# Fewer TensorE instructions and 1 MB transfers in the two later passes of a Fourier layer

## The chip, the cores and the metric

The kernel runs on one core of one Trainium2 chip. The core has TensorE for matrix products (its weight loads are listed as PEld beside the matmuls, PE), VectorE (DVE), ScalarE (ACT), GpSimd (POOL) and SyncE (SP), an on-chip memory of 128 partitions, and a smaller one, PSUM, that TensorE writes and VectorE and ScalarE read. Sixteen DMA engines move data between on-chip memory and HBM; instructions on SP, ACT and POOL issue the transfers. The metric is the device time of one execution in microseconds, smaller is better.

## The reference

Images of 256 x 256 points (64 of them) go through a Fourier neural operator with 32 channels and four layers; its output, joined with 77 text rows, goes through attention and a feed-forward layer. The change lies in the four layers:

```python
v = jnp.transpose(h @ p_w + p_b, (0, 3, 1, 2))            # 64 x 32 x 256 x 256
for i in range(4):
    x_ft = jnp.fft.rfft2(v)                               # 12 x 24 modes are kept
    x1 = irfft2(modes of x_ft, mixed over channels by fw1[i], fw2[i])
    x2 = jnp.einsum('bcxy,cd->bdxy', v, w_w[i]) + w_b[i]
    v = x1 + x2
    v = (v - mean) * rsqrt(var + eps) * bn_g[i] + bn_b[i] # mean, var over images and points
    if i < 3: v = relu(v)
out = einsum('bcxy,cu->bxyu', v, q_w) + q_b
```

Everything is fp32. The mean and variance are taken over all images, so that each layer needs a pass over all data before the next can normalise.

## The kernel before

An image's activation v is 32 channels x 65,536 points, 8 MB, and lives in HBM in two sets of buffers (`vd`), as eight chunks of 1 MB: 128 partitions x 8 rows x 256 values. `layer` (line 546) is one pass over the 64 images. It is called three times, with i = 0, 1, 2; between passes `mix` (line 428) multiplies the kept modes by the weights. In pass 0 nothing is loaded but the small input image; in passes 1 and 2, "the later passes", every chunk is loaded from one set of buffers and stored to the other.

For image b and chunk t a pass has these steps, each a small function of `layer`:

- `am` (643): SP loads the mixed modes of image b (`ams`), and POOL scales them in place (`scale_am`, 631).
- `sp`, `spT` (658, 667): inverse transform along x on PE, then a transpose on DVE into `y`.
- `ld` (652): load of the chunk into `vin`, four buffers.
- `pre` (676): on PE, the inverse transform along y (line 682, 8 products of 256 columns) plus the channel product of the loaded chunk (line 693, 16 products on 32 x 32 tiles of the array, 512 columns each), into two PSUM tiles.
- `evA`, `evB` (700): each evicts one of the two PSUM tiles with relu into `vo`, four buffers; the letter `a` or `d` behind the point picks ACT (705) or DVE (707).
- `st` (711): store of the chunk `vo`.
- `turn` (716): DVE transposes the chunk for the forward transform.
- `prod` (724): PE multiplies the chunk by the next layer's channel weights (line 730, 16 products on 32 x 32 tiles), and `sqA`, `sqB` (736) let ACT square and sum the result, for the variance.
- `y0` to `y7` (745): forward transform along y on PE (752), one eighth of it each; `half`, `zt0`, `zt1` (759, 765) move and transpose the result.
- `x` (778): forward transform along x on PE: 12 products with full 128 x 128 weights taken from `zt` and 96 columns of the table FX (line 786). `xo` (795) copies the result, `xs` (802) has SP store it.

An fp32 product is two pairs of weight load and matmul in the profile.

The order of all steps is written out by hand in two strings, `ORDER[0]` for pass 0 and `ORDER[1]` for the later passes (line 128). A word such as `evA2.a@1` is step evA for chunk 2 of image b+1, on ACT; the loop at line 824 walks the string once for each b. Each engine executes its instructions in this order. PSUM is four tiles called `ring`: `pre`, `prod` and `y` take two each, `sp` and `x` one, and `close` frees them in order. Both `ld` and `st` split a chunk in two halves of 512 KB, and both are issued on SP, hence into one queue. Waits are put in by the framework: a load waits for the product that read its buffer's former content, an eviction for the store of its buffer's former content.

The lines of the steps above that matter most in what follows:

```python
nc.sync.dma_start(vin[b, t][:, rows], src[b][:, t, rows])       # 656, twice per chunk
nc.sync.dma_start(dst[b][:, t, rows], vo[b, t][:, rows])        # 714, twice per chunk
for k in range(4):                                              # 727, prod
    for n in range(4):
        j = (n + k) % 4
        nc.tensor.matmul(ps[n][32 * j:32 * j + 32], lhsT=w4[i + 1][32 * n:32 * n + 32], ...)
```

Of the kernel before, what the change touches and what calls it, by code (L numbers as in the profile page):

```python
# [9 lines left out]
F32 = mybir.dt.float32  # L10
# [7 lines left out]
C = 32  # L18
M = 12
KX = 2 * M  # L20
# [14 lines left out]
def _tables():  # L35
# [92 lines left out]
ORDER = [(  # L128
# [7 lines left out]
), (  # L136
# [7 lines left out]
)]  # L144

_TABLES, _GRIDS = _tables()
# [7 lines left out]
def tile_fno_fusion_transformer(ctx: ExitStack, tc: tile.TileContext, a, cst_d, grid_d, out):  # L154
    nc = tc.nc
    x = a["x"].rearrange("b x y o -> b x (y o)")
# [3 lines left out]
    const = ctx.enter_context(tc.tile_pool(name="const", bufs=1))  # L160
# [15 lines left out]
    T4, ID, ONES, CHAN = tab("t4"), tab("ident"), tab("ones"), tab("chan")  # L176

    CROW = tab("crow").rearrange("p (n k) -> p n k", n=4)

    epsc = const.tile([128, 1], F32, name="epsc")  # L180
    nc.vector.memset(epsc, EPS)

# [29 lines left out]
    w4 = [w4all[:, i, :] for i in range(L)]  # L212
# [333 lines left out]
    def layer(i, st, src, dst, acc):  # L546
# [3 lines left out]
        EX, FX = EXL[lay], FXL[lay]  # L550
# [3 lines left out]
        with ExitStack() as cx:  # L554
            def pool(name, bufs, **kw):
                return cx.enter_context(tc.tile_pool(name=name, bufs=bufs, **kw))

            ip = pool("li", 2 if i == 0 else 4, reuse_waits="tile")
            op, yp, cp, xp, zp, tp = (
                pool(n, k, reuse_waits="tile")  # L560
                for n, k in (("lo", 4), ("ly", 1), ("lc", 1), ("lx", 2), ("lz", 1), ("lt", 6))
            )
# [20 lines left out]
            for n in range(nr):  # L583
# [4 lines left out]
                if n:  # L588
                    nc.vector.tensor_add(a0, a0, a1)
            nc.vector.tensor_copy(ams[1], ams[0])  # L590
            ws = cp.tile([128, C], F32, name="ws")
            if i:
                nc.vector.tensor_mul(ws, w4[i], s_)
            if i == 0:
                mv = [ip.tile([128, 4, 4 * S + 8], F32, name="mv") for n in range(2)]
                mv = [t[:, :, 0:4 * S].rearrange("p q (s y) -> p q s y", s=4) for t in mv]
                for t in mv:
                    nc.sync.dma_start(t, grid_d.rearrange("p (q s y) -> p q s y", q=4, s=4))

            ring, free, clock = {}, [0] * 4, [0]  # L600

            def take(key, n):

                clock[0] += 1
                mine = sorted((k for k in range(4) if free[k] >= 0), key=lambda k: free[k])[:n]
                for k in mine:
                    free[k] = -1
                ring[key] = [(k, pp.tile([128, 2, 512], F32, name=f"ring{k}")) for k in mine]
                return [t for _, t in ring[key]]

            def banks(key):
                return [t[:, n] for _, t in ring[key] for n in range(2)]

            def close(key, n):

                clock[0] += 1
                free[ring[key][n][0]] = clock[0]

            y_, t32, vin, vo, half_, zts = {}, {}, {}, {}, {}, {}
# [31 lines left out]

            def ld(b, t, e):
                vin[b, t] = ip.tile([128, 8, S], F32, name="vin")
                for n in range(2):
                    rows = slice(4 * n, 4 * n + 4)
                    nc.sync.dma_start(vin[b, t][:, rows], src[b][:, t, rows])

            def sp(b, h, e):
                ps = take(("sp", b, h), 1)[0]
# [49 lines left out]
                return run  # L709

            def st_(b, t, e):
                for n in range(2):
                    rows = slice(4 * n, 4 * n + 4)
                    nc.sync.dma_start(dst[b][:, t, rows], vo[b, t][:, rows])
# [9 lines left out]
            def prod(b, t, e):  # L724
                take(("prod", b, t), 2)
                ps = banks(("prod", b, t))
                for k in range(4):
                    for n in range(4):
                        j = (n + k) % 4
                        nc.tensor.matmul(  # L730
                            ps[n][32 * j:32 * j + 32], lhsT=w4[i + 1][32 * n:32 * n + 32],
                            rhs=vo[b, t][32 * n:32 * n + 32, 2 * j:2 * j + 2, :], start=True, stop=True,
                            skip_group_check=True, tile_position=(32 * n, 32 * j),
                        )

            def sq(n):
                def run(b, t, e):
                    key = "prod", b, t
                    at = 2 * (8 * b + t) + n
                    ps = ring[key][n][1]  # L740
                    nc.scalar.activation(ps, ps, AF.Square, accum_out=acc[:, at:at + 1])  # L741
                    close(key, n)
                return run
# [21 lines left out]
            def zt(h):  # L765
                def run(b, n, e):
                    if b not in zts:
                        zts[b] = zp.tile([128, 2, 32, C], F32, name="zt")
                    whole = h == 0 or b not in half_
                    nc.vector.transpose(  # L770
                        zts[b][:, h].rearrange("p k c -> p c k"),
                        (ring["y", b][h][1] if whole else half_[b]).rearrange("p n (s c) -> p c (n s)", c=C),
                    )
                    if whole:
                        close(("y", b), h)
                return run

            def x_(b, n, e):
                zt_ = zts.pop(b)
                ps = take(("x", b), 1)[0]  # L780
                for g in range(3):
                    n = 0
                    for h in range(2):
                        for r in range(2):
                            k0 = M * r + 4 * g
                            nc.tensor.matmul(  # L786
                                ps[:, 0, 96 * g:96 * g + 96],
                                lhsT=zt_[:, h, k0:k0 + 4, :].rearrange("p k c -> p (k c)"),
                                rhs=FX[:, h, 48 * r:48 * r + 96], start=n == 0, stop=n == 3,
                            )  # L790
                            n += 1

            xos = {}

            def xo(b, n, e):
                xos[b] = xp.tile([128, 3, 2 * KX], F32, name="xo")
                nc.scalar.copy(
                    xos[b], ring["x", b][0][1][:, 0, 0:288].rearrange("p (g k) -> p g k", g=3)[:, :, 0:2 * KX]
                )
                close(("x", b), 0)  # L800

            def xs(b, n, e):
                nc.sync.dma_start(xh_d[i][:, b, :], xos.pop(b).rearrange("p g k -> p (g k)"))

            run = dict(
                am=am, lx=lx, ld=ld, sp=sp, spT=spT, pre=pre, evA=ev(0), evB=ev(1), st=st_, turn=turn,
                prod=prod, sqA=sq(0), sqB=sq(1), y=y, half=half, zt0=zt(0), zt1=zt(1), x=x_, xo=xo, xs=xs,
            )
            steps = []
            for word in ORDER[min(i, 1)].split():  # L810
                word, _, late = word.partition("@")
                word, _, e = word.partition(".")
                name = word if word in run else word.rstrip("0123456789")
# [48 lines left out]
    src = vd[L % 2]  # L862
# [50 lines left out]
    with tc.tile_pool(name="tw", bufs=1) as tp, tc.tile_pool(name="tq", bufs=2, space=PSUM) as tq:  # L913
# [5 lines left out]
        for dh in range(2):  # L919
            ps = tq.tile([128, D], F32, name="wtp")  # L920
# [5 lines left out]
        for l, r, d_ in ((wn["q"], wn["k"], wqk), (wn["v"], woT, wvE[:, :, 0:D])):  # L926
            for dh in range(2):
                ps = tq.tile([128, D], F32, name="wtp")
                for eh in range(2):
                    nc.tensor.matmul(  # L930
                        ps, lhsT=l[:, eh, 128 * dh:128 * dh + 128], rhs=r[:, eh, :],
                        start=eh == 0, stop=eh == 1,
                    )
                evict(d_[:, dh, :], ps)
        for dh in range(2):
            ps = tq.tile([128, D], F32, name="wtp")
            for eh in range(2):
                nc.tensor.matmul(
                    ps[:, 0:1], lhsT=wn["k"][:, eh, 128 * dh:128 * dh + 128], rhs=bcol["q"][:, eh, :],
                    start=eh == 0, stop=eh == 1,  # L940
# [4 lines left out]
        ps = tq.tile([128, D], F32, name="wtp")  # L945
# [4 lines left out]
    rows = [128, 128, TXT]  # L950
# [283 lines left out]
```

## Time and profile before

| | us |
|---|---|
| median of 3 runs | 11281.18 (11275.21 to 11285.59) |
| the profiled execution | 11293.58 |
| its span | 11291.7 |
| PE busy | 10625.0 (94%) |
| DVE busy | 8446.5 (75%) |
| ACT busy | 6473.1 (57%) |
| POOL busy | 1442.4 (13%) |

The page cuts the span into 40 equal slices; each digit is the busy share of a slice in tenths, and the last row gives what the DMA engines moved:

```profile
PE   6999999998999999999799999999996999999999
DVE  6888888887777777777677777777775666666665
DMA  6776676678999999999899999999998555555553
GB/s 213 247 250 244 249 247 248 246 253 320 383 376 382 380 377 372 374 379 379 305 375 380 380 376 378 381 380 376 372 379 291 226 227 228 227 227 228 226 227 140
```

Pass 0 fills slices 1 to 8, the two later passes slices 9 to 29 (the dips at 19 and 30 are the mixing between them), and the transformer with its own loads of v the rest. DMA engines read and write at about 380 GB/s in the later passes. Matmuls are pipelined and their ends are modelled in the trace, so PE's share says less than the other rows.

### The profile page before, as it was taken

How to read it: one execution, taken by the hardware profiler on the slowest of the kernel's cores; microseconds unless marked ns; L12 is line 12 of the kernel's file. 1: busy time of each engine (PE TensorE's matmuls, PEld its weight loads, DVE VectorE, ACT ScalarE, POOL GpSimd, SP SyncE). 2: the span in 40 equal slices, each digit the busy share in tenths (PEclk: the TensorE clock that was granted, in tenths of full speed). 3: DMA queues.
4: the chain of work that ended last, by engine and by line, in shares of the span. 5: the costliest groups of instructions: out<-in, count | busy, mean ns of one | idle time of the engine just before them, and what ended most of it. 6: DMA issues, size and time to landing. Idle time of an engine off the chain costs nothing.

```text
span 11291.7 us, 409300 instructions
## 1 busy us (share of the span) xinstructions
PE 10625.0 (94%) x182550; PEld 5738.0 (51%) x182550; DVE 8446.5 (75%) x10381; ACT 6473.1 (57%) x10673; POOL 1442.4 (13%) x2179
## 2 busy tenths in 40 slices
PE   6999999998999999999799999999996999999999
PEld 3555555554444444444444444444443666666666
DVE  6888888887777777777677777777775666666665
ACT  5777777775566655566555566655563333333333
POOL 1111111110000000000000000000000333333333
PEclk8999999998999999999899999999998999999999
DMA  6776676678999999999899999999998555555553
GB/s 213 247 250 244 249 247 248 246 253 320 383 376 382 380 377 372 374 379 379 305 375 380 380 376 378 381 380 376 372 379 291 226 227 228 227 227 228 226 227 140
DMA packets 972544, 3457.29 MB, mean 306 GB/s; under 512 B 149784, under 2 KB 199320, under 8 KB 903832
## 3 DMA queue, kind: packets, MB, share of 16 engines
q1 hardware_dynamic: 905344, 3366.80, 77.8%
q0 software_dynamic: 58288, 60.60, 2.3%
q8 instruction: 1428, 23.40, 0.8%
q10 hardware_dynamic: 7144, 3.72, 0.1%
q14 instruction: 340, 2.79, 0.1%
HBM read 1733.60 MB, written 1696.92 MB: 304 GB/s over the span
## 4 chain that ended last, share of the span: by engine, by line
PE 62%; DMA 20%; DVE 9%; ACT 3%; issue 3%; SPq 2%; POOL 0%; ACTq 0%; DVEq 0%; POOLq 0%
PE ring L752 15%; DMA v<-vo 11%; PE ring L682 9%; PE ring L730 8%; DMA vin<-v 6%; PE ring L693 5%; PE hp L982 4%; PE ring L662 3%; PE pp L1145 3%; PE pp L1156 3%; PE ring L786 2%; DVE vo L707 2%; PE pp L1110 2%; PE pp L1175 2%; PE pp L1072 1%
## 5 line engine op out<-in xcount | busy, mean ns | idle before, releaser
L741 ACT ACTIVATE ring<-ring 128x1024 f32<-128x1024 f32 x3072 | 3115.8, 1014 | 1188.4 <-PE ring L730 1119.5
L719 DVE STREAM_TRANSPOSE t<-vo 128x2048 f32<-128x2048 f32 x1536 | 3465.7, 2286 | 20.9 <-DVE vo L707 0.9
L730 PE MATMUL ring<-vo,w 32*32 32x512 f32 x49152 | 2413.1, 600 | 85.0 <-ACT vo L705 68.3
L707 DVE TENSOR_SCALAR vo<-ring 128x1024 f32<-128x1024 f32 x1280 | 1544.5, 1221 | 1199.7 <-PE ring L693 806.6
L705 ACT ACTIVATE vo<-ring 128x1024 f32<-128x1024 f32 x1792 | 1791.7, 1023 | 1044.1 <-PE ring L693 500.9
L752 PE MATMUL ring<-t,cst 32*32 32x512 f32 x49152 | 2072.0, 599 | 51.0 <-issue 44.9
L752 PEld LDWEIGHTS ring<-t,cst 32*32 32x32 f32 x49152 | 913.4, 103 | 925.6 <-issue 622.6
L730 PEld LDWEIGHTS ring<-vo,w 32*32 32x32 f32 x49152 | 803.2, 103 | 1070.2 <-issue 407.1
L693 PE MATMUL ring<-vin,ws 32*32 32x512 f32 x32768 | 1287.8, 603 | 22.9 <-issue 16.2
L682 PE MATMUL ring<-cst,y 24*128 24x256 f32 x16384 | 1230.3, 402 | 77.0 <-DVE vo L707 61.7
L682 PEld LDWEIGHTS ring<-cst,y 24*128 24x128 f32 x16384 | 789.5, 185 | 993.2 <-DVE vo L707 392.4
L631 POOL TENSOR_TENSOR ams<-ams,bns 48x512 f32<-48x512 f32 x384 | 400.5, 1043 | 6989.4 <-DMA ams<-mix 6510.1
L670 DVE STREAM_TRANSPOSE y<-ring 128x1024 f32<-128x1024 f32 x384 | 763.1, 1987 | 329.5 <-PE ring L662 328.5
L682 PE MATMUL ring<-mv,y 29*128 29x256 f32 x8192 | 705.3, 403 | 36.3 <-ACT ring L741 19.6
L682 PEld LDWEIGHTS ring<-mv,y 29*128 29x128 f32 x8192 | 456.9, 185 | 369.0 <-ACT ring L741 209.3
L786 PEld LDWEIGHTS ring<-cst,zt 128*128 128x128 f32 x4608 | 533.6, 193 | 177.1 <-ACT vo L705 114.2
L762 ACT COPY half<-ring 128x1024 f32<-128x1024 f32 x192 | 194.4, 1013 | 731.4 <-PE ring L752 731.4
L1183 POOL DMA_DIRECT2D out_dram<-o x1024 | 508.2, 505 | 659.0 <-DVE o L1178 616.9
L741 ACT ACTIVATION_READ_ACCUMULATOR ring<-ring 128x1 f32 x3072 | 585.6, 191 | 0.0
L786 PE MATMUL ring<-cst,zt 128*128 128x96 f32 x4608 | 565.6, 280 | 6.1 <-DVE zt L770 5.7
L770 DVE STREAM_TRANSPOSE zt<-ring 128x1024 f32<-128x1024 f32 x192 | 377.4, 1965 | 248.1 <-PE ring L752 248.1
L662 PE MATMUL ring<-ams,cst 49*128 49x512 f32 (+1 forms) x1536 | 450.6, 642 | 99.1 <-POOL ams L631 37.2
(374 smaller groups left out, 9762.6 us busy)
## 6 DMA issues: line engine op xcount, KB each, us to landing
v<-vo SPq DMA_DIRECT2D x3072, 512.0 KB, 7.8
vin<-v SPq DMA_DIRECT2D x2048, 512.0 KB, 9.1
ch<-v SPq DMA_DIRECT2D x512, 1024.0 KB, 12.5
mix<-ob SPq DMA_DIRECT2D x96, 512.0 KB, 5.6
ams<-mix SPq DMA_DIRECT2D x384, 96.0 KB, 8.0
xin<-in_x_dram SPq DMA_DIRECT2D x16, 1024.0 KB, 6.5
mv<-in_x_dram POOLq DMA_DIRECT2D x256, 64.0 KB, 7.4
out_dram<-o POOLq DMA_DIRECT2D x1024, 16.0 KB, 3.0
```

The source lines that it names most:

```text
L662: nc.tensor.matmul(ps[:, n, :], lhsT=EX[hv, 128 * h:128 * h + 128], rhs=ams[b % 2][hv], start=True, stop=True, skip_group_check=True,)
L670: nc.vector.transpose(y_[b, h].rearrange("p q c -> p c q"), ring[key][0][1].rearrange("p n (c k) -> p (n c) k", k=32),)
L682: nc.tensor.matmul(ps[n][:, 256 * r:256 * r + 256], lhsT=y_[b, t // 4][32 * n:32 * n + K, q:q + 4, :].rearrange("p q c -> p (q c)"), rhs=m ...
L693: nc.tensor.matmul(ps[n][32 * j:32 * j + 32], lhsT=ws[32 * n:32 * n + 32], rhs=v[32 * n:32 * n + 32, 2 * j:2 * j + 2, :], start=False, sto ...
L705: nc.scalar.activation(to, ring[key][h][1], AF.Relu)
L707: nc.vector.tensor_scalar(to, ring[key][h][1], 0.0, None, ALU.max)
L719: nc.vector.transpose(t32[b, t // 2][:, :, 8 * (t % 2):8 * (t % 2) + 8, :].rearrange("p y s c -> p s y c"), vo[b, t].rearrange("p s (y l) ...
L730: nc.tensor.matmul(ps[n][32 * j:32 * j + 32], lhsT=w4[i + 1][32 * n:32 * n + 32], rhs=vo[b, t][32 * n:32 * n + 32, 2 * j:2 * j + 2, :], st ...
L741: nc.scalar.activation(ps, ps, AF.Square, accum_out=acc[:, at:at + 1])
L752: nc.tensor.matmul(ps[n][32 * j:32 * j + 32], lhsT=FYT[32 * n:32 * n + 32, k, :], rhs=t32[b, j][32 * n:32 * n + 32, k].rearrange("p s c -> ...
L786: nc.tensor.matmul(ps[:, 0, 96 * g:96 * g + 96], lhsT=zt_[:, h, k0:k0 + 4, :].rearrange("p k c -> p (k c)"), rhs=FX[:, h, 48 * r:48 * r + ...
L1183: nc.gpsimd.dma_start(out[b, 64 * n + 16 * g:64 * n + 16 * g + 16].rearrange("(p t) d -> p t d", t=2), o[32 * g + 8 * n:32 * g + 8 * n + 8 ...
```

## The change

Only passes 1 and 2 are touched, apart from two small tables.

- A chunk is loaded by one 1 MB transfer on SP instead of two of 512 KB.
- A chunk is stored by one 1 MB transfer, issued on GpSimd instead of SP.
- The x transform takes its weights from the table FX and streams `zt` through the array: 4 products of 384 columns, each into 64 PSUM partitions. The result then lies the other way round; `xe` copies it to on-chip memory and `xt` turns it with 3 products against `ID2`, two stacked unit matrices that also add the two halves.
- Two of an image's eight `prod` steps (chunks 1 and 7, marked `.w`) use 8 products on 64 x 64 tiles with the block-diagonal weights `w64`, instead of 16 on 32 x 32 tiles.
- `ORDER[1]` is written anew.

```diff
-    "pre5 sqB7@-1 zt1@-1 sqA7@-1 pre6 evA5.a ld2@1 st4 evB5.d st5 turn4 evA6.a prod5 x@-1 "
-    "evB6.a sqB5 prod6 sqA5 xo@-1 turn5 pre2@1 sqA6 turn6 sqB6 prod4 evA2.a@1 evB2.d@1 "
-    "sqB4 ld0@1 ld7 sqA4 pre0@1 evB0.d@1 ld3@1 prod2@1 st6 evA0.a@1 turn2@1 sqB2@1 sqA2@1 "
-    "pre3@1 ld1@1 evA3.a@1 st2@1 evB3.d@1 pre7 evB7.d prod3@1 ld5@1 evA7.a sqA3@1 turn7 "
-    "pre1@1 st0@1 am@2 sqB3@1 prod0@1 evA1.a@1 evB1.d@1 sqA0@1 st7 sp1@1 st1@1 ld4@1 y0 "
-    "spT1@1 y1 ld6@1 turn0@1 turn3@1 xs@-2 y2 sqB0@1 prod1@1 y3 sqB1@1 sp0@2 y4 sqA1@1 "
-    "spT0@2 y5 y6 st3@1 turn1@1 y7 half.a pre4@1 zt0 prod7 evB4.d@1 evA4.a@1 "
+    "evB2.a@1 ld5 ld7 pre4 ld0@1 turn6 evA2.a@1 prod6 evA4.a x@-1 evB4.d xe.d@-1 turn4 "
+    "sqB6 prod4 xt@-1 st2@1 sqA6 turn2@1 sqA4 pre5 xo@-1 sqB4 am@2 evA5.d evB5.a pre3@1 "
+    "prod2@1 evA3.d@1 turn5 evB3.a@1 st4 xs@-1 sqA2@1 pre7 sqB2@1 evA7.a prod5 evB7.d "
+    "sqB5 pre0@1 st5 ld1@1 sqA5 prod3@1 turn7 evB0.a@1 sp1@1 sqA3@1 evA0.d@1 pre1@1 "
+    "sqB3@1 spT1@1 evA1.a@1 prod0@1 sqA0@1 ld6@1 evB1.d@1 ld2@2 st3@1 sp0@2 spT0@2 y0 "
+    "ld4@1 y1 st1@1 sqB0@1 turn3@1 turn0@1 pre6@1 y2 y3 evA6.a@1 y4 evB6.a@1 prod1.w@1 "
+    "sqB1@1 st7 sqA1@1 y5 st0@1 y6 st6@1 turn1@1 y7 prod7.w half.a zt0 sqA7 sqB7 ld3@2 "
+    "zt1 pre2@2 "
...
+    ID2 = const.tile([128, 2 * KX], F32, name="id2")
+    nc.vector.tensor_add(ID2, ID[:, 0:2 * KX], ID[:, 64:64 + 2 * KX])
...
+            w64 = cp.tile([128, 2, C], F32, name="w64")
+            nc.vector.memset(w64, 0.0)
+            for n in range(4):
+                nc.vector.tensor_copy(w64[32 * n:32 * n + 32, n % 2, :], w4[i + 1][32 * n:32 * n + 32])
+            w64 = w64.rearrange("p n o -> p (n o)")
...
             def ld(b, t, e):
-                for n in range(2):
-                    rows = slice(4 * n, 4 * n + 4)
-                    nc.sync.dma_start(vin[b, t][:, rows], src[b][:, t, rows])
+                nc.sync.dma_start(vin[b, t], src[b][:, t])
...
             def st_(b, t, e):
+                if i:
+                    nc.gpsimd.dma_start(dst[b][:, t], vo[b, t])
+                    return
...
             def prod(b, t, e):
+                if e == "w":
+                    for j in range(4):
+                        for n in range(2):
+                            m = (n + j) % 2
+                            nc.tensor.matmul(
+                                ps[j][64 * m:64 * m + 64], lhsT=w64[64 * n:64 * n + 64],
+                                rhs=vo[b, t][64 * n:64 * n + 64, 2 * j:2 * j + 2, :], start=True, stop=True,
+                                skip_group_check=True,
+                            )
+                    return
...
             def x_(b, n, e):
+                if turned:
+                    for r in range(2):
+                        for h in range(2):
+                            nc.tensor.matmul(
+                                ps[64 * h:64 * h + 64, 0, 0:384], lhsT=FX[:, h, 48 * r:48 * r + 64],
+                                rhs=zt_[:, h, M * r:M * r + M, :].rearrange("p k c -> p (k c)"),
+                                start=r == 0, stop=r == 1, skip_group_check=True,
+                            )
+                    return
...
+            def xe(b, n, e):
+                xes[b] = xp.tile([128, 384], F32, name="xe")
...
+                    nc.vector.tensor_copy(xes[b], ring["x", b][0][1][:, 0, 0:384])
+
+            def xt(b, n, e):
+                xe_ = xes.pop(b)
+                for g in range(3):
+                    nc.tensor.matmul(
+                        ring["x", b][0][1][:, 1, 96 * g:96 * g + 2 * KX],
+                        lhsT=xe_[:, 128 * g:128 * g + 128], rhs=ID2, start=True, stop=True,
+                    )
```

`xo` copies its 288 columns from the PSUM tile's other bank when the transform is turned. In pass 0 all steps stay as they were.

More of the change, by code (lines that the diff above doesn't have):

```diff
@@ L598, in layer @@
                     nc.sync.dma_start(t, grid_d.rearrange("p (q s y) -> p q s y", q=4, s=4))
+            turned = "xt" in ORDER[min(i, 1)]
             ring, free, clock = {}, [0] * 4, [0]
@@ L791, in x_ @@
                             n += 1
-            xos = {}
+            xos, xes = {}, {}
+            def xe(b, n, e):
+                xes[b] = xp.tile([128, 384], F32, name="xe")
+                if e == "a":
+                    nc.scalar.copy(xes[b], ring["x", b][0][1][:, 0, 0:384])
+                else:
+                    nc.vector.tensor_copy(xes[b], ring["x", b][0][1][:, 0, 0:384])
[6 more added lines that the diff above has]
+                    )
             def xo(b, n, e):
@@ L797, in xo @@
                 nc.scalar.copy(
-                    xos[b], ring["x", b][0][1][:, 0, 0:288].rearrange("p (g k) -> p g k", g=3)[:, :, 0:2 * KX]
+                    xos[b], ring["x", b][0][1][:, int(turned), 0:288].rearrange("p (g k) -> p g k", g=3)[:, :, 0:2 * KX]
                 )
@@ L806, in layer @@
                 am=am, lx=lx, ld=ld, sp=sp, spT=spT, pre=pre, evA=ev(0), evB=ev(1), st=st_, turn=turn,
-                prod=prod, sqA=sq(0), sqB=sq(1), y=y, half=half, zt0=zt(0), zt1=zt(1), x=x_, xo=xo, xs=xs,
+                prod=prod, sqA=sq(0), sqB=sq(1), y=y, half=half, zt0=zt(0), zt1=zt(1), x=x_, xe=xe,
+                xt=xt, xo=xo, xs=xs,
             )
```

## The prediction

> **What bounds the kernel now.** I began with the forty slices on the page: one stage, slices 9 to 29, runs with the DMA share at nine tenths. These are the two later passes (lines 546 to 827 with i = 1 and 2), the only ones the change alters. Next I asked for busy time by window, for one steady window of each stage. Columns: window, length, busy us and instruction count of TensorE (PE), its weight loads (PEld), VectorE (DVE), ScalarE (ACT), GpSimd (POOL), then clock, DMA share, GB/s.
>
> ```profile
> core 0: us, PE busy (x) PEld busy (x) DVE busy (x) ACT busy (x) POOL busy (x), PEclk, DMA share, GB/s
> 3000.00:5000.00 2000.00, 1915.77 (x40768) 902.98 (x40766) 1496.18 (x835) 1199.22 (x1888) 91.91 (x88) 1.00 0.98 377
> 300.00:2400.00 2100.00, 2042.04 (x38758) 1073.14 (x38758) 1867.73 (x1039) 1600.59 (x2536) 248.25 (x346) 1.00 0.70 247
> ```
>
> First row, a later pass: DMA 0.98 and PE 96% at once. Second row, the first pass: PE is 97% "busy" with a third less DMA, so a busy PE here proves little (matmul ends are modelled), while 16 engines at 98% cannot be pressed further. Of x transforms 44 fall into the 2000 us, so one image takes 45.45 us; 2 passes x 64 images make 128 images, and **1 us per image is 128 us**.
>
> The DMA view and the waits of the same window:
>
> ```profile
> q1 hardware_dynamic: 214437, 749.15, 96.9%
> vin<-v SPq DMA_DIRECT2D x704, 512.0 KB, 9.0
> v<-vo SPq DMA_DIRECT2D x702, 512.0 KB, 8.9
> ams<-mix SPq DMA_DIRECT2D x88, 96.0 KB, 8.6
> ```
> ```profile
> ACT vo L705 <- DMA v<-vo: 95.7, 71, 3.0
> DVE vo L707 <- DMA v<-vo: 94.3, 72, 3.0
> PEld ring L693 <- DMA vin<-v: 9.0, 18, 1.0
> POOL ams L631 <- DMA ams<-mix: 1861.2, 43, 46.1
> ```
>
> One queue carries everything, and a half-chunk takes 9 us to land though its bytes alone need 1.3 us: a deep queue. Evictions wait for a vo buffer whose store is still under way, (95.7 + 94.3) / 44 = 4.3 us per image; both halves of a chunk wait together, so about 2.2 us of path. Loads are almost never waited for. The chain of waits over one image, however, stays on PE:
>
> ```profile
> by line: PE ring L682 22.9%; PE ring L693 21.7%; PE ring L752 21.2%; PE ring L730 17.1%; PE ring L786 6.5%; DVE vo L707 5.5%; PE ring L662 5.2%; issue 1.1%
> ```
>
> So two limits lie close together. From the matmul records, time from the start of a group to the next one's, at its tenth percentile: L682 1.08 us, L693 0.88, L730 1.07, four y groups 4.44, x 2.85, sp 1.06. Per image 8 x (1.08 + 0.88 + 1.07) + 2 x 4.44 + 2.85 + 2 x 1.06 = 38.1 us of PE, 7.3 under the period. DMA: the window's packets sum to 44.5 us per image, 0.9 under it. DMA is the tighter.
>
> **1 MB transfers.** A chunk row of 4 KB is now 8 KB. Packet records of the window: 4096 B take 159 ns at the median, 168.1 in the mean. Per image 4096 of them: 4096 x 168.1 / 16 engines = 43.0 us. No 8192 B packet flows in this stage. Nearest row for the loads: ch in the last stage, SyncE, 1 MB, same rows: 313 ns median, 320.4 mean. For the stores: xh, loaded through GpSimd in 32,256 B packets of 1194 ns; with 159 for 4096 that is 27.2 B/ns plus 8.5 ns a packet, so 309.6 ns for 8192. Under load either the excess of 9 ns stays per packet (318.6) or it grows in proportion (327). Savings per image, 2048 x (336.2 - t) / 16: 2.25 us at 318.6, 1.18 at 327; 0.6 if only the loads get long packets. I take 1.18, since the ch row was measured in an unsaturated stage, and add the 16 dropped DMAs, a 9 ns completion packet on each engine: 0.14. Together **1.3 us**.
>
> The Trainium skill ("DMA: Bandwidth & Descriptors", Measured) says to batch to 1 MiB for 75% of peak, with about 2.0 us fixed plus bytes / 436 GB/s per DMA. By that, 32 half-MB DMAs would take 32 x 3.2 = 102 us per image and 16 whole ones 71; the trace has 45.45 and 377 GB/s already. The fixed part is covered by the queue here; only the packet's 8.5 ns counts.
>
> **Stores on GpSimd.** The same page ("Issuing engines are not separate DMA queues") speaks against a gain: all issuers share 16 engines and only sequencer time is saved. I agree: SP is freed of 16 issues and of its waits for evictions (368.4 us, 8.4 per image), but loads were waited for only 9 us in all, so that is worth nothing. The cost on POOL is this row:
>
> ```profile
> L845 POOL DMA_DIRECT2D xh<-xh x3: 552/552/557, 2532.8 to 8569.7; - x3
> ```
>
> 0.55 us each, 8 per image = 4.4 us, beside 2.1 us of scaling in 45: idle time. But POOL runs in order, and `am` makes it wait for the ams loads before it scales; `st4` and `st5` now queue behind. That is new:
>
> ```profile
> 5042.03 1.56 SPq L623 DMA_DIRECT2D ams<-mix  x2
> ```
> ```profile
> 5051.63 2.17 POOL L631 TENSOR_TENSOR ams<-ams,bns 48x512 f32<-48x512 f32 x2 [42.67 <-DMA ams<-mix]
> ```
>
> Issue to end of scaling is 11.8 us. In the new order SP issues `am` right after `ld0`, which waits for `pre4`; so `st4` leaves at about pre4 + 12.4. Its vo buffer is wanted by the fourth next chunk, `pre0`: between lie prod6, x, prod4, xt, pre5, pre3, prod2, pre7, prod5, pre0, about 14.6 us at the floors, 17.4 at the stage's ratio 45.45 / 38.1. If the store lands within 5 us nothing is lost; in 6.4 us (1 MB at half the rate, 5.1, plus the 1.3 by which the fastest half-chunk, 2.6, exceeds its bytes) 1.4 are exposed; with today's 8.9, 3.9. Bounds 0 to 3.9. I take 0: freed of stores, the queue ahead of ams is shorter, and work-conserving engines load meanwhile.
>
> **x transform.** 24 matmul instructions (12 fp32 products of two passes each) in 2.85 us go. Added: 4 products of 384 columns on half the array's columns, two side by side, and 3 turns of 48 columns against ID2. The 512-column passes step by 0.43 us, so 384 take 0.32; two pairs x two passes = 1.28, plus a 0.2 us switch. The turns are 6 instructions at 2.85 / 24 = 0.12: 0.7, plus 0.2. Together 2.4: **0.45 saved**. `xe.d` is a 384-column PSUM read on DVE, by L707 (1.22 us for 1024) 0.5 us; DVE gives one eviction to ACT (7 to 6 on DVE), so is less loaded; prod4 stands between xe and xt and hides it; without that cover PE would lose the 0.5.
>
> **Two wide products.** 16 instead of 32 matmuls each, but only four 64x64 tiles work at once instead of sixteen: 4 rounds x 0.43 = 1.71 us against 1.07. The tiling page ("TensorEngine Tiling (Array Packing)", Key Properties) adds that changing the mode drains the array; the rows price that: sp needs 2 rounds x 0.43 = 0.85 and takes 1.06, so 0.2 each way. By rounds alone +0.64, with drains +1.04 each. Against it: narrow groups run at 1.07 where their stream needs 0.85, that is 64 instructions at 16.7 ns, so PE is bound by issue there; 32 fewer give back 0.53 if they queue up behind the wide one. Between +0.1 and +1.04; I take 0.5 each, +1.0 per image. PE in sum: +0.55 on 38.1. It lies in PE's 7.3 us of slack except where a ring waits behind it: 0.2 counted.
>
> **Order, tables.** The order is written anew; both sides keep four buffers. SP now issues only loads, ams and xs: each `ld` still waits for the chunk four places earlier (ld0 for pre4, ld1 for pre3, ld6 for pre5), and no longer behind an eviction. Before, a load took 9.0 us to land from a queue that it shared; after, ld5 leaves before pre4 and pre5 starts some 6 us later (prod6, x, prod4, xt: 4.9 at the floors), with one load ahead instead of a mixed queue. Bounds: the 9 us that loads cost in 44 images, 0.2 each, could go (gain 0.2), or pre5 could wait 9.0 - 6 = 3 us; nearest is the L693 row, so 0. The earlier `pre2@2` adds one chunk of run-in: under 3 us per pass. ID2 and w64 are a handful of VectorE instructions per pass: under 2 us in all.
>
> **Sum.** 1.3 - 0.2 = 1.1 us per image x 128 = **141 us**. The profiled execution took 11293.6 (span 11291.7 and 1.9 around it): 11153. It lies 12.4 above the median 11281.2, so against that: **11140**.
>
> **Rivals.**
> A, the forecast: DMA paces the stage. For it: 0.98 and the waits for stores. Against: the chain never leaves PE and VectorE. 11140; own range 0.4 to 2.2 us per image: 11000 to 11230. Chance 0.47.
> B, PE's order binds: the relief is unused, wide products cost up to their drains, 2.1 - 0.45 = 1.6 us, about half hidden, 0.8: 11281 + 102 = 11383; with all hidden, no change. For it: the chain. Against: 7.3 us of slack, and PE stops on evictions that wait for stores. Chance 0.15.
> C, slower: `st4` and `st5` stuck behind the scaling, vo comes free late, pre0 and pre1 wait. Exposed 1.4 to 3.9, middle 2.6, less 1.1 gained = +1.5 us: 11281 + 192 = 11473. It decides the sign from 1.1 us exposed. For it: the 11.8 us, and stores are already what is waited for. Against: while stores are held, the engines serve loads, and a backlog is made up at full rate. Chance 0.38.
>
> Only 0.2% can be told from no change, 23 us. Faster takes A (0.47); the same gets 0.08 from B and C's edge; slower 0.45. The range reaches from A's stronger half to most of C: 11010 to 11440.
>
> **What would show it.** Packets of 8192 B in both queues near 320 ns and a DMA share under 0.98 with a shorter period show the first step. "vo <- DMA v<-vo" per image under 4.3 us favours A, over it C, with POOL's stores starting right after the scaling. Groups of wide products: 1.7 to 2.1 us; x and turns 2.4. Period near 44.3 us. I am wrong if packets stay 4 KB, or if the period rises with POOL's stores bunched.

## The result and the profile after

The changed kernel takes 12466.97 us in the median of 4 runs (12459.09 to 12470.66), the kernel before 11279.12 beside it: ratio 1.1051, 95% interval 1.1038 to 1.1065. It is **10.5% slower**; 141 us less had been forecast, 1188 more came. Over 128 images of the later passes that is 9.3 us each.

The page after, in the forty slices (counted from 0):

```profile
PE   6999999978888888888788888888888799999999
DMA  6767676778888888888788888888887755555553
```

The later passes now fill slices 9 to 31 of a longer span. PE and DMA both fell from 9 to 8 there: neither of the two is what sets the time now. The same steady window as before, with the same columns:

```profile
3000.00:5000.00 2000.00, 1682.91 (x32040) 715.40 (x32027) 1200.87 (x689) 1023.06 (x1594) 228.76 (x363) 0.91 0.82 312
```

POOL executes ten instructions per image (eight stores, two scalings), so 363 of them are 36.3 images: 55.1 us per image, where it was 45.45. The clock is down to 0.91. Then the DMA view of the window (packets, MB and share; issues with the median from issue to landing) and its waits (us in total, times, longest):

```profile
q1 hardware_dynamic: 51579, 314.06, 43.7%
q0 software_dynamic: 41904, 305.15, 37.8%
...
v<-vo POOLq DMA_DIRECT2D x291, 1024.0 KB, 10.4
vin<-v SPq DMA_DIRECT2D x290, 1024.0 KB, 6.2
ams<-mix SPq DMA_DIRECT2D x72, 96.0 KB, 9.5
```
```profile
ACT vo L712 <- DMA v<-vo: 288.4, 37, 10.4
DVE vo L714 <- DMA v<-vo: 282.8, 37, 10.2
PE ring L689 <- ACT vo L712: 274.2, 37, 9.9
POOL ams L640 <- DMA ams<-mix: 272.2, 33, 10.7
```

The transfers did what they say: 8192 B packets in both queues, 309 ns at the median. But evictions wait for a store once per image, 288.4 / 36.3 = 7.9 us of it; both halves of the chunk wait at the same time, and PE (L689) waits behind them. One image in the timeline (start, length, engine and line; in brackets the idle time before and what ended it):

```profile
5026.22 0.53 POOL L720 DMA_DIRECT2D v<-vo  x1 [14.83 <-ACT vo L712]
5026.54 0.89 SPq L632 DMA_DIRECT2D ams<-mix  x2
...
5036.20 2.16 POOL L640 TENSOR_TENSOR ams<-ams,bns 48x512 f32<-48x512 f32 x2 [9.45 <-DMA ams<-mix]
...
5037.99 1.16 PE L700 MATMUL ring<-vin,ws 32*32 32x512 f32 x32
...
5038.32 1.64 POOL L720 DMA_DIRECT2D v<-vo  x3
...
5045.89 1.02 ACT L712 ACTIVATE vo<-ring 128x1024 f32<-128x1024 f32 x1 [6.66 <-DMA v<-vo]
5045.90 1.22 DVE L714 TENSOR_SCALAR vo<-ring 128x1024 f32<-128x1024 f32 x1 [6.85 <-DMA v<-vo]
...
5046.97 2.29 PE L689 MATMUL ring<-cst,y 24*128 24x256 f32 x16 [6.54 <-ACT vo L712]
...
5049.19 2.01 PE L700 MATMUL ring<-vin,ws 32*32 32x512 f32 x32
```

`st2` leaves, SP issues the load of `ams`, and GpSimd stands still for 9.45 us until it lands. Chunk 4 has been in `vo` since 5027.4, but `st4`, `st5` and `st3` leave only behind the scaling, in one bunch at 5038.32: a ready store was held 10.9 us. Chunk 7's products (5037.99) are done at 5039.15, and its evictions wait until 5045.9, when the first store of the bunch has landed. Then two PE groups take 2.29 and 2.01 us instead of the 1.15 and 1.16 that the same lines take elsewhere in this image. The windows around the wait give the reason (the last three numbers are clock, DMA share, GB/s):

```profile
5036.00:5040.00 4.00, 4.00 (x111) 1.62 (x93) 3.06 (x2) 2.84 (x5) 3.68 (x5) 1.00 1.02 420
5040.00:5044.00 4.00, 0.42 (x15) 0.00 (x0) 0.00 (x0) 0.00 (x0) 0.00 (x0) 1.00 1.00 369
5044.00:5047.00 3.00, 0.03 (x2) 0.04 (x2) 1.10 (x1) 1.11 (x2) 0.00 (x0) 0.57 1.00 401
5047.00:5049.00 2.00, 2.00 (x16) 1.54 (x16) 1.90 (x2) 1.97 (x4) 0.00 (x0) 0.50 1.02 430
5049.00:5050.00 1.00, 1.00 (x20) 0.28 (x32) 0.54 (x1) 0.00 (x0) 0.00 (x0) 0.50 1.01 426
5050.00:5051.00 1.00, 1.00 (x33) 0.27 (x2) 0.00 (x0) 0.00 (x0) 0.00 (x0) 0.50 0.61 246
5051.00:5052.00 1.00, 1.00 (x48) 0.46 (x31) 0.65 (x1) 0.59 (x1) 0.00 (x0) 0.88 0.10 41
```

All engines are still while the DMA engines work at full rate; the clock drops to 0.50 and stays there until about 5051; and when the bunch and the queued loads are through, the DMA engines in turn have nothing to do (0.10): loads wait for buffers that only a running PE frees (in the window SP's load instructions wait 1698.4 us in all for PE's channel products, line 700).

### The profile page after: what moved, and what is told of

It reads as the page before. It is cut to its first block, busy times and chain, and to the rows that moved or that the text cites. A ratio compares the mean times of both kernels' runs of the same rounds, so it can differ in the third digit from the quotient of the medians.

```text
span 12463.5 us, 394621 instructions
## 1 busy us (share of the span) xinstructions
PE 10980.0 (88%) x177174; PEld 5617.4 (45%) x177174; DVE 8338.7 (67%) x10397; ACT 6593.1 (53%) x10801; POOL 1989.6 (16%) x3203
## 5 line engine op out<-in xcount | busy, mean ns | idle before, releaser
L712 ACT ACTIVATE vo<-ring 128x1024 f32<-128x1024 f32 x1920 | 1917.6, 1023 | 2642.7 <-PE ring L700 1472.3
L714 DVE TENSOR_SCALAR vo<-ring 128x1024 f32<-128x1024 f32 x1152 | 1391.8, 1217 | 1529.3 <-DMA v<-vo 920.0
L689 PE MATMUL ring<-cst,y 24*128 24x256 f32 x16384 | 1420.1, 436 | 933.2 <-ACT vo L712 877.9
L750 PE MATMUL ring<-vo,w 32*32 32x512 f32 x40960 | 1931.4, 623 | 29.6 <-ACT vo L712 28.1
L689 PEld LDWEIGHTS ring<-cst,y 24*128 24x128 f32 x16384 | 911.4, 201 | 1769.5 <-ACT vo L712 993.9
L720 POOL DMA_DIRECT2D v<-vo x1024 | 549.5, 541 | 5009.6 <-ACT vo L712 4892.9
L772 PEld LDWEIGHTS ring<-t,cst 32*32 32x32 f32 x49152 | 849.8, 103 | 1103.9 <-issue 746.4
L750 PEld LDWEIGHTS ring<-vo,w 32*32 32x32 f32 x40960 | 663.4, 105 | 922.1 <-issue 495.9
L689 PE MATMUL ring<-mv,y 29*128 29x256 f32 x8192 | 702.5, 402 | 36.9 <-ACT ring L761 19.8
L689 PEld LDWEIGHTS ring<-mv,y 29*128 29x128 f32 x8192 | 454.2, 184 | 370.2 <-ACT ring L761 212.8
L741 PE MATMUL ring<-vo,w 64*64 64x512 f32 x4096 | 521.8, 610 | 8.0 <-issue 6.7
L1027 PE MATMUL hp<-ch,win 128*32 128x512 f32 x4096 | 471.8, 601 | 7.4 <-DMA ch<-v 7.2
## 6 DMA issues: line engine op xcount, KB each, us to landing
ch<-v SPq DMA_DIRECT2D x512, 1024.0 KB, 12.4
```

The source lines that it names most:

```text
L689: nc.tensor.matmul(ps[n][:, 256 * r:256 * r + 256], lhsT=y_[b, t // 4][32 * n:32 * n + K, q:q + 4, :].rearrange("p q c -> p (q c)"), rhs=m ...
L712: nc.scalar.activation(to, ring[key][h][1], AF.Relu)
L714: nc.vector.tensor_scalar(to, ring[key][h][1], 0.0, None, ALU.max)
L720: nc.gpsimd.dma_start(dst[b][:, t], vo[b, t])
L741: nc.tensor.matmul(ps[j][64 * m:64 * m + 64], lhsT=w64[64 * n:64 * n + 64], rhs=vo[b, t][64 * n:64 * n + 64, 2 * j:2 * j + 2, :], start=Tr ...
L772: nc.tensor.matmul(ps[n][32 * j:32 * j + 32], lhsT=FYT[32 * n:32 * n + 32, k, :], rhs=t32[b, j][32 * n:32 * n + 32, k].rearrange("p s c -> ...
```

## The experiments

The ratio is always to the kernel before, run beside each experiment (its medians lie between 11279 and 11284 us); differences between two medians are divided by 128 images.

**e1: the scaling behind the stores.** `am` in the later passes only loads; a new word `sm` scales behind `st3`, three stores further on in GpSimd's queue.

```diff
-    "... evB1.d@1 ld2@2 st3@1 sp0@2 ..."
+    "... evB1.d@1 ld2@2 st3@1 sm@2 sp0@2 ..."
             def am(b, n, e):
                 if b > 1:
                     load_am(b)
-                    scale_am(b)
+                    if not i:
+                        scale_am(b)
+            def sm(b, n, e):
+                if b > 1:
+                    scale_am(b)
```

> The changed kernel with the scaling of ams moved, in the later passes, from its place at am@2 (ahead of st4 and st5 on GpSimd) to a place behind st3@1; the load stays where it is. Held stores (GpSimd waits 7.5 us per image for the ams load, three stores behind it leave together and evictions wait for them): the stall of 7.8 us per image goes, period about 46 us, time 11,250 to 11,500. Slow stores (a 1 MB store from GpSimd takes 10.4 us to land wherever it stands): no more than 2 us per image gained, time above 12,200. Slow order or wide products: the same, above 12,200.

11236.75 us, ratio 0.9961 (0.9946 to 0.9976). The whole loss is gone, 9.6 us per image, and a small gain stands. Window and waits as above:

```profile
3000.00:5000.00 2000.00, 1967.88 (x39571) 844.28 (x39570) 1481.97 (x847) 1262.00 (x1961) 283.20 (x444) 1.00 0.96 383
```
```profile
POOL v L725 <- DMA ams<-mix: 19.3, 13, 1.6
ACT vo L717 <- DMA v<-vo: 14.8, 17, 2.2
```

GpSimd's timeline over one image:

```profile
5000.44 0.53 POOL L725 DMA_DIRECT2D v<-vo  x1 [13.29 <-ACT vo L717]
5002.15 0.53 POOL L725 DMA_DIRECT2D v<-vo  x1 [1.18 <-DVE vo L719]
5009.57 0.53 POOL L725 DMA_DIRECT2D v<-vo  x1 [6.89 <-DVE vo L719]
5011.59 0.53 POOL L725 DMA_DIRECT2D v<-vo  x1 [1.48 <-PE ring L755]
5012.19 2.16 POOL L640 TENSOR_TENSOR ams<-ams,bns 48x512 f32<-48x512 f32 x2
```

`st2`, `st4`, `st5` and `st3` leave one by one as their chunks come. The scaling comes 11.75 us behind `st2`, where it came 9.98 behind it before: hardly later in time, but with nothing held and hardly a wait of its own (19.3 us in the whole window). 44.4 images, 45.05 us each; the clock is 1.00 and evictions wait 0.3 us per image.

The balance of the loss, 55.1 - 45.05 = 10.05 us per image, has two parts. PE stands still longer: from its busy time in the two windows, (2000 - 1682.91) / 36.3 = 8.7 us per image against (2000 - 1967.88) / 44.4 = 0.7, so 8.0 more. And PE works at half clock for a while: the clock records of the trace show 9.5 us per image at 0.50, in 5.6 of which PE is busy, and half of that is lost, an estimate of 2.8 (e1 has none). In the image shown the second part is smaller, 1.14 + 0.85 = 2.0. Together 10.8, slightly more than the whole.

**e5: a dose.** The scaling between `st4` and `st5`, so that `st4` is free and `st5` and `st3` are held.

```diff
-    "... evB3.a@1 st4 xs@-1 ..."
+    "... evB3.a@1 st4 sm@2 xs@-1 ..."
```

> Dose: the changed kernel with the scaling between st4 and st5, so that st4 leaves freely and st5 and st3 are held. Held stores: pre0 no longer waits, but pre1 wants the buffer of st5, which leaves about 4 us late, so a part of the stall comes back, some 1 to 4 us per image over the 44.8 of the first experiment: 11,350 to 11,750. If any place of the scaling but the original one were harmless (a peculiarity of that one place): 11,230 to 11,250.

11499.01, ratio 1.0193 (1.0177 to 1.0208): 2.0 us per image over e1, with 142.2 us of waits in 42.4 images, 3.4 each. Holding the later stores costs a fifth of holding the first.

**e9: the other end of the wait.** Scaling stays ahead of `st4`, but SP issues the load one round of the order earlier (`al@3` behind `st3@1`).

```diff
-    "... ld2@2 st3@1 sp0@2 ..."
+    "... ld2@2 st3@1 al@3 sp0@2 ..."
```

> The changed kernel with the scaling where the change has it, ahead of st4 and st5 on GpSimd, but with the load of ams issued some 25 us earlier (behind st3 of the image before), so that it has landed when GpSimd gets to the scaling. If the wait for the landing holds the stores: only the 2.2 us of scaling stand ahead of st4, time 11,220 to 11,350, as with the scaling moved. If the scaling itself in this place, or something else that the first experiment moved, were the cause: above 12,000.

11292.93, ratio 1.0010 (1.0004 to 1.0017): 9.2 of the 9.6 us return, though GpSimd's order is the one that held the stores. Not the scaling's 2.16 us but the wait for landing is what the stores paid for.

**e12, e13: which buffer?** By the semaphores in the trace chunk 7's evictions wait for `st4` and chunk 0's for `st2`, though with four buffers in turn 7 would follow 2 and 0 follow 4. Why the framework hands them out so is not shown. Two attempts to change that by moving the word `st4` behind `pre7` or behind `evB7`:

```diff
-    "... evB3.a@1 st4 xs@-1 sqA2@1 pre7 sqB2@1 evA7.a prod5 evB7.d ..."
+    "... evB3.a@1 xs@-1 sqA2@1 pre7 st4 sqB2@1 evA7.a prod5 evB7.d ..."     # e12
+    "... evB3.a@1 xs@-1 sqA2@1 pre7 sqB2@1 evA7.a prod5 evB7.d st4 ..."     # e13
```

> The changed kernel with the word st4 moved from ahead of pre7 to behind it. GpSimd's own sequence stays the same (scaling, st4, st5, st3), so the hold stays; but when pre7 takes its vo buffer, chunk 4 is no longer given back, and pre7 should get chunk 2's buffer, whose store left 12 us earlier. If the size of the stall comes from pre7 taking the very buffer of the held st4: pre7 runs on, pre0 waits instead and later, some 4 us of the stall go, and the time falls to 11,450 to 12,050. If it does not matter which buffer is taken: 12,400 to 12,500.

> As the run before, but with st4 behind evB7, since the trace of that run shows the eviction of chunk 7 still waiting for the store of chunk 4: the buffer seems to be given out at the first write, evA7, ahead of which st4 still stood. GpSimd's sequence is again the same. If the buffer that chunk 7 gets sets the size of the stall: evA7 gets chunk 2's buffer and runs on, pre0 waits instead, some 4 us per image of the stall go, 11,450 to 12,050. If the choice of buffer has nothing to do with the words' order: 12,400 to 12,500.

12482.38 (1.1062, 1.1044 to 1.1081) and 12481.06 (1.1069, 1.1051 to 1.1088): nothing moved. On GpSimd `st4` still stands between the scaling and `st5`, so e13's sequences on GpSimd and SyncE are those of the changed kernel, and in both traces the evictions still wait for the store of the bunch. A word moved past work of other engines alone may change nothing; the question stayed open until e14.

**e14, e15: buffers in turn.** Four named `vo` tiles, used one after the other; e14 keeps the scaling ahead of `st4`, e15 has it late as in e1.

```diff
-                for n, k in (("lo", 4), ...
+                for n, k in (("lo", 1 if i else 4), ...
...
-                vo[b, t] = op.tile([128, 8, S], F32, name="vo")
+                nth[0] += 1
+                vo[b, t] = op.tile([128, 8, S], F32, name=f"vo{nth[0] % 4}" if i else "vo")
```

> The changed kernel, scaling in its place, with the four vo buffers given out strictly in turn in the later passes (four named tiles). Chunk 7 then gets the buffer of chunk 2, whose store left 12 us before the held ones, and chunk 0 that of chunk 4. If the size of the stall comes from chunk 7 taking the held store's buffer: the wait moves to pre0, about 4 us per image go, 11,450 to 12,050. If not: 12,350 to 12,500.

> The first experiment (scaling later, 11,237) with the vo buffers given out in turn: the control for the run before. Evictions hardly wait for stores there (0.6 us per image), so 11,210 to 11,270; a larger move would say that the hand-out matters by itself.

e14: 11990.31, ratio 1.0643 (1.0616 to 1.0671), 3.7 us per image less than the changed kernel with the same hold. The wait has moved to the next chunk, 0. Its window, its waits, and clock windows around one such wait:

```profile
3000.00:5000.00 2000.00, 1828.58 (x34886) 766.72 (x34887) 1302.49 (x746) 1108.30 (x1727) 248.08 (x394) 0.95 0.88 338
...
5022.00:5024.00 2.00, 1.73 (x56) 0.50 (x31) 0.64 (x1) 0.25 (x2) 0.00 (x0) 1.00 1.09 410
5024.00:5026.00 2.00, 0.17 (x2) 0.17 (x4) 1.23 (x1) 1.25 (x2) 0.00 (x0) 1.00 0.92 369
5026.00:5028.00 2.00, 2.00 (x12) 0.83 (x16) 0.64 (x1) 1.83 (x4) 0.00 (x0) 0.62 1.05 438
5028.00:5030.00 2.00, 2.00 (x32) 0.80 (x40) 1.28 (x1) 0.00 (x0) 0.00 (x0) 0.50 0.98 406
5030.00:5032.00 2.00, 2.00 (x49) 0.78 (x32) 0.54 (x1) 0.59 (x1) 0.00 (x0) 0.50 1.05 442
5032.00:5034.00 2.00, 2.00 (x36) 0.30 (x4) 0.69 (x1) 1.04 (x2) 0.79 (x2) 0.67 0.94 360
```
```profile
ACT vo L713 <- DMA v<-vo: 144.8, 42, 5.7
```

39.4 images wait 3.7 us each, and after a PE pause of only some 2 us the clock is low for about 7. e15, with neither hold nor early reuse, takes **11214.43**, ratio 0.9936 (0.9922 to 0.9951), below both kernels, though its interval overlaps that of e1. It is 6.1 us per image under e14. PE is idle 4.35 us per image in e14's window and 0.61 in e15's, which is 3.7 of them; by the clock records e14 has PE busy at half clock for 5.2 us per image and e15 never, an estimate of 2.6 lost. The two make 6.3.

**e2, e3, e4, e8: the transfers alone.** e3 and e4 are the kernel before with 1 MB loads on SP and 1 MB stores on SP (e3) or GpSimd (e4). e2 is the changed kernel with its 1 MB stores on SP; e8 has both transfers in halves on SP, as before.

```diff
-                for n in range(2):
-                    rows = slice(4 * n, 4 * n + 4)
-                    nc.sync.dma_start(vin[b, t][:, rows], src[b][:, t, rows])
+                nc.sync.dma_start(vin[b, t], src[b][:, t])
...
+                if i:
+                    nc.sync.dma_start(dst[b][:, t], vo[b, t])      # e4: nc.gpsimd
+                    return
```

> The changed kernel with its 1 MB stores issued on SyncE at the same words of the order; all else stays. Held stores: SyncE never waits for the ams load, so the stores leave when their data is there, unless a load ahead of them waits for its buffer; time 11,200 to 11,600. Slow stores: also 11,200 to 11,600, so this run alone does not part the two. Slow order or wide products: the stall stays, above 12,200.

> The kernel before with whole-chunk loads and stores of 1 MB, both on SyncE, its own order, x transform and products. If DMA time is what paced the stage before, 8 KB packets (309 instead of 159 + 159 ns) save 0.7 to 1.3 us per image: 11,110 to 11,190. If TensorE's order paced it, no change, 11,260 to 11,300; a store that waits for both evictions instead of one could cost up to 1 us per image, 11,410.

> The kernel before with the change's transfers alone: 1 MB loads on SyncE, 1 MB stores on GpSimd, its own order. Held stores: am@2 stands ahead of st7 and st1 here too, GpSimd holds them some 7 us, and the time rises by 3 to 9 us per image, to 11,700 to 12,400. Slow stores: rises as well, with evictions waiting at every chunk and not once per image. Slow order or wide products: no rise, 11,100 to 11,300.

> The changed kernel with the transfers of before (halves of 512 KB, loads and stores on SyncE): order, x transform and wide products alone. If DMA time paces the stage: its packets take 44.5 us per image again, at 98% 45.4: 11,280 to 11,320, against 11,280 for whole chunks on SyncE. If TensorE's order paces it: within 30 us of the 11,280 of whole chunks on SyncE, at a DMA share near 0.98.

e2: 11280.52, 0.9997 (0.9988 to 1.0006). e3: 11306.41, 1.0019 (1.0010 to 1.0029). e4: 11307.33, 1.0023 (1.0015 to 1.0031). e8: 11311.25, 1.0025 (1.0015 to 1.0035). In e3's window the long packets relieve the DMA engines:

```profile
3000.00:5000.00 2000.00, 1906.90 (x40558) 896.19 (x40540) 1490.51 (x831) 1192.71 (x1877) 91.97 (x88) 1.00 0.94 375
```

The DMA share goes from 0.98 to 0.94, and 88 scalings are still 44 images in 2000 us: the period has not moved. **Shorter DMA time alone gains nothing.** Two things keep this from naming PE as the one bound. With whole chunks PE also waits longer for loads, so that a gain may have been spent there (before, this row had 9.0 us, 18 times):

```profile
PEld ring L691 <- DMA vin<-v: 34.3, 37, 1.7
```

And e8, with the new order, the new x transform and the wide products on the transfers of before, gains nothing either, at the DMA share and the rate of before:

```profile
3000.00:5000.00 2000.00, 1937.92 (x38952) 830.32 (x38935) 1459.62 (x836) 1239.96 (x1932) 91.91 (x88) 0.99 0.98 377
```

Its 11311 lies in the range that its expectation gave for DMA time, and a little outside the one for PE's order. Relief of DMA alone (e3) and of PE alone (e8) each bring nothing; with both, e2 equals the kernel before and e1 is 0.4% faster. The two limits lay close together, and which of them paced the kernel before is not settled.

In the new order 1 MB on SP instead of halves is worth 11311.25 - 11280.52 = 31 us, and issuing the stores on GpSimd, once nothing waits ahead of them, another 44 (e2 to e1). And e4 warns of reading a wait by its length: there GpSimd waits for `ams` as well, 437.9 us or about 10 per image, and it costs next to nothing.

```profile
POOL ams L631 <- DMA ams<-mix: 437.9, 46, 11.5
```

**e10: the hold put into the old order.** e4 with `am@2` moved ahead of `st4`.

```diff
-    "pre5 ... ld2@1 st4 evB5.d st5 ... st0@1 am@2 sqB3@1 ..."
+    "pre5 ... ld2@1 am@2 st4 evB5.d st5 ... st0@1 sqB3@1 ..."
```

> The kernel before with the change's transfers (11,307 when am@2 stands ahead of st7) and am@2 moved ahead of st4, in front of chunks that follow one another closely. If a held store costs time only where the next chunks soon want its buffer: GpSimd waits about 10 us per image as it did there, but evictions now wait and the time rises by 3 to 9 us per image, to 11,700 to 12,450. If the change's order had some other fault: stays at 11,290 to 11,330.

11359.96, ratio 1.0068 (1.0053 to 1.0083), 0.4 us per image over e4, and far under what was expected. Its timeline:

```profile
5029.05 1.50 SPq L623 DMA_DIRECT2D ams<-mix  x2
...
5043.23 1.22 DVE L705 TENSOR_SCALAR vo<-ring 128x1024 f32<-128x1024 f32 x1 [0.38 <-PE ring L691]
...
5044.59 2.17 POOL L631 TENSOR_TENSOR ams<-ams,bns 48x512 f32<-48x512 f32 x2 [15.02 <-DMA ams<-mix]
...
5046.70 0.61 POOL L711 DMA_DIRECT2D v<-vo  x1
```

GpSimd stood 15 us, but SP had issued the load ahead of the y steps; the chunk to be stored was evicted only at 5044.4, so a ready store was held 2.3 us and not 15. By these runs (10.9 us held and 9.6 lost, 2.3 held and 0.4 lost) what counts is how long a ready store stands.

**e6, e7, e11: the PE parts, each on e1.** e6 has narrow products for chunks 1 and 7 again, e7 the old x transform, e11 a third wide product.

```diff
-    "... prod1.w@1 ... prod7.w ..."
+    "... prod1@1 ... prod7 ..."                # e6
-    "... x@-1 evB4.d xe.d@-1 ... xt@-1 ..."
+    "... x@-1 evB4.d ..."                      # e7
-    "... prod0@1 ..."
+    "... prod0.w@1 ..."                        # e11
```

> The first experiment with the two wide products narrow again. Wide costs (array rounds and drains, 1.88 against 1.07 us, nothing comes back): 2 x 0.8 x 128 = 205 us faster, 11,030. Wide pays (32 fewer instructions at 16.7 ns each, 0.53 us): 2 x 0.53 x 128 = 136 us slower, 11,370. Both in balance or hidden: within 30 us of 11,237.

> The first experiment with the x transform of before (12 products of 96 columns, no copy and no turn). The new transform takes 1.44 + 0.80 = 2.24 us on TensorE, the old one 2.85. If TensorE paces the stage: 0.6 us per image slower, 11,315. If it hides in waits: within 30 us of 11,237. If the copy on VectorE and the second stop of the ring tile cost more than is saved: below 11,200.

> The first experiment (11,237) with a third wide product, prod0 ahead of the y groups. Two wide products were worth 117 us, 0.46 us per image each. If each saves issue time wherever narrow groups follow: 11,180. If only two places have the queue for it: 11,230 to 11,300.

e6: 11354.17, 1.0070 (1.0055 to 1.0085), 117 us over e1: each wide product gains 0.46 us, 0.92 per image, though it takes 1.88 us from its start to the next group and a narrow one 1.07. The longer stream is not free; it costs 2 x 0.81 = 1.6 us per image. But with narrow products PE stands still more, (2000 - 1876.06) / 43.4 = 2.86 us per image against 0.72 in e1, and most of that is "issue", time in which PE waited for nothing that the profile shows, ahead of the y groups (L777) and the narrow products (L755). The first two rows are e6, the third is e1:

```profile
PE ring L777 <- issue: 69.4, 46, 3.1
PE ring L755 <- issue: 25.0, 19, 2.8
PE ring L777 <- issue: 8.3, 15, 0.9
```

Some of these pauses bring the clock down as well: by the clock records e6 runs 30.7 us of the window at half clock and e1 none, an estimate of 0.3 us per image. In sum 2.1 - 1.6 + 0.3 = 0.8 us, close to the 0.92. Why PE pauses there is not shown.

e7: 11413.59, 1.0124 (1.0107 to 1.0141), 177 us or 1.38 us per image over e1. e11: 11239.60, 0.9962 (0.9948 to 0.9977), no further gain.

## Why the prediction was wrong

**Where it failed.** The step is "Bounds 0 to 3.9. I take 0" for the exposed wait behind the scaling. The mechanism of rival C is what happened, with its first term right: "`st4` leaves at about pre4 + 12.4" - it left 12.4 us after pre4's products (5025.96 to 5038.32). Two terms were wrong, and a third was missing:

- "Its vo buffer is wanted by the fourth next chunk, pre0", 17.4 us later. It was wanted by the third next, chunk 7, at 5039.15: 13.2 us. That buffers go round in turn was assumed, never read. With the landing 7.5 us after the issue (inside the bounds of 5 to 8.9) the exposure is 12.4 + 7.5 - 13.2 = 6.7 us in this image, where ACT stands 6.66; the mean over the window is 7.9. e14 tests the sum the other way: in turn it gives 12.4 + 7.5 - 17.4 = 2.5 us. There ACT waits 2.50 in the image shown, which is closer than the sum deserves, and 3.7 in the mean. The difference of the two means, 4.2 us, is the one that the buffer makes in the sum, 17.4 - 13.2.
- The reason given for 0, that "the queue ahead of ams is shorter, and work-conserving engines load meanwhile": `ams` landed in 9.5 us, not sooner than the 8.6 before, and the DMA engines did work meanwhile (share 1.00), but then ran out of loads (0.10), since loads wait for a PE that stands. The mean share fell to 0.82, so the lost time was not made up.
- No term stood for the clock. The pauses of PE are followed by stretches at half clock, worth about 2.8 us per image here (estimated under e1).

So C's 11473 was 1.5 us per image above the median, and the run 9.3. The bounds of 0 to 3.9 are too low by the 4.2 us of the buffer, the one term in them that no row stood behind, and by the clock.

**The premise.** "DMA is the tighter" was to turn shorter packets into a shorter period, and did not: in e3 the DMA share fell by four points without a gain. The 1.3 us per image "saved" were real as packet time: 309 ns at the median against 309.6 worked out, but 323 for stores and 363 for loads in the mean after, and 312 and 336 in e1. A DMA share of 0.98 did not mean that DMA alone set the time; the chain of waits, which never left PE and VectorE, had pointed to PE. But e8 shows that PE's relief alone was not enough either, so "two limits lie close together" was the part that held. The 2.0 us per DMA that the prediction quotes from the Trainium skill ("DMA: Bandwidth & Descriptors"), and then sets aside, belong on that page to transfers issued from GpSimd; those of the kernel before were on SyncE.

**The PE parts.** That PE's order binds was rival B's premise, but the wide products were priced with the wrong sign: a cost of 0.5 us each against a measured gain of 0.46. The longer stream was sized rightly (0.64 to 1.04 us against 0.81); what was missed is how much PE pauses around the narrow ones. The x transform was to save 0.45 us; the group takes 1.44 and the turns 0.80, 2.24 in place of 2.85, so 0.61 directly, and e7 gives 1.38. Why more than its own PE time comes back is not settled; the order was written around the shorter form. The parts do not add up: e1 gains 42 us, though taking back x, the wide products or the issue on GpSimd alone loses 44 to 177 each.

**What held.** A store takes GpSimd 0.53 us (0.55 worked out); loads were hardly waited for (0.4 us in e1's whole window); the signs named for C, stores bunched right after the scaling and more wait for `vo` than the 4.3 us per image before (571.2 / 36.3 = 15.7, both halves counted), were the ones seen. That SP's relief "is worth nothing" was 44 us off.

## What to carry to other kernels

Before stores are put on an engine that executes in order, look for an instruction on it that waits for a load, and measure how long a *ready* store would stand behind it and when its buffer is next written; which chunk writes it next has to be read from the semaphores, not assumed from the number of buffers. One word of order decided between 10.5% slower and 0.4% faster here; giving the buffers out in turn added perhaps another 0.2%, which is hardly clear of the noise. A DMA share near 1 does not make DMA the only bound: shorten its packets' time alone, then the other engine's work alone, and see which of the two the period follows. Here it followed neither.

## What was not expected of the hardware

A pause of PE lowered the clock for longer than it lasted. In e14 PE paused for some 2 us (from 5023.7, where its last group's modelled end lies, to 5025.83), and the granted clock was 0.62, 0.50, 0.50 and 0.67 in the next four windows of 2 us: by the clock records of the trace it was at half from 5026.49 to 5033.32, with PE busy throughout. In the changed kernel, after a pause of 6.5 us, it was at half from 5044.42 to 5051.25, of which the last 4.3 us were with PE busy again. Both stretches last 6.83 us, and every stretch at half clock in the two 2000 us windows is one to four times 3.41 us long.

The Trainium skill ("TensorE: Matmul & The Clock Gate", What's actually happening) puts the drop to half at an idle window of about 3.4 us and the return after as long a busy one. The half rate, the unit of time and the changed kernel, with the drop 4.0 us after PE stopped and the return 4.3 us after it went on, agree with that. The pause that tripped it in e14 is shorter than that figure, and the clock came back only after 7.5 us of busy PE: here the measurement decides. So a wait on PE's path can cost more than its length: e14 has 3.7 us per image more of PE standing still than e15 and is 6.1 slower.
